# Expert tiles 36 to 38 of a mixture-of-experts layer put behind a test of the filled count

## The chip, the core and the metric

The kernel runs on one core of a Trainium2 chip, as one program. The metric is the device time of one execution in microseconds (us), lower is better. Times come from several executions of the same program; beside them one execution was recorded by the hardware profiler, and all views below are of that one.

The engines of a core run side by side and each works through its own queue of instructions: TensorE (PE; its loads of weights are shown as PEld), VectorE (DVE), ScalarE (ACT), GpSimd (POOL) and SyncE (SP). They wait for each other through semaphores. An engine's sequencer (shown with a q, POOLq) reads the queue and handles waits, register instructions and branches itself.

## What is computed

Input are 2048 tokens of 512 numbers, all in float32. Layer normalisation, a Mamba-2 block, a gated MLP, and then the part that matters here, a mixture of 8 experts of which each token uses two:

```python
x = x + _L0_attn_ref(_layernorm(x), ...)          # Mamba-2 and MLP
x = x + _L0_ffn_ref(_layernorm(x), Wr, Wg, Wu, Wd)

# _L0_ffn_ref, H = 512, I = 352, E = 8, K = 2
probs = softmax(x @ Wr)
topk_w, topk_idx = top_k(probs, K)
topk_w = topk_w / sum(topk_w)
g, u = x @ Wg[e], x @ Wu[e]
y[e] = (silu(g) * u) @ Wd[e]
out = sum over the token's two experts of weight * y[e]
```

The reference computes every expert for every token. The kernel computes a token's two experts alone.

## The kernel before

The work runs in blocks of tokens. The Mamba part (`mamba`, eight blocks of 256 tokens) and the MLP (`feed_forward`, four blocks of 512) are woven into each other; TensorE's order is the order of the program (`tc.manual_schedule` on PE, left by `in_order.close()` at line 1111). Each MLP block ends with `route`, which writes the normalised rows to memory (`xnd`, and `xnd1` for the first 1536 tokens), picks the two experts of each token and enters the tokens into a list for each expert.

**The tables.** An expert's list is cut into tiles of 128 tokens, and only as many tiles as it has are worked on. How many that is depends on the data, so the program lays out a fixed number, `NS`, and a table says which expert and which list a tile belongs to. The most that 4096 entries in eight lists can fill is `NS = (2 * T + NE * (P - 1)) // P` = 39 (line 38). `table` (line 924) is called twice:

- Table 1, for `NS1` = 10 tiles, after the first 1536 tokens. It counts full tiles only, so that these ten can be computed while the last MLP block still runs.
- Table 2, for the other `NS - NS1` = 29 tiles, after all tokens. Here an expert's tiles are its count over 128, rounded up, less those already used.

`upto_e` (line 939) is the running sum of tiles over the experts, so its last column is the number of tiles that the table fills. `exp_i` (lines 957 to 959) holds each tile's expert as an integer. A tile past the last list gets expert 7 and no tokens: its gather reads rows `T` to `T + 127`, which hold zeros, and its scatter adds zeros to the same spare rows of `out`. Such a tile takes the same instructions as a filled one.

**One expert tile** is these steps:

- `gather` (line 1012): POOL issues an indirect DMA that brings 128 rows into `xg`.
- `front` (1020): TensorE transposes them (`pt`, four matmuls, line 193) and ACT copies the result to `xgT` (line 195).
- `hidden` (1025): TensorE's sequencer reads the expert's number from `exp_i` (line 1027), and gate and up are computed from the weights in `ew` (line 1034). ACT takes the Silu (1038), DVE the product (1039).
- `turned` (1042): transposes of the product (`pht`), copied by DVE and ACT.
- `back` (1052): the down projection (`epd`, line 1055), scaled by the token's weight on DVE (`ey`, line 1060), and an indirect DMA from POOL that adds the rows to `out` (line 1061). Each such scatter waits for the one before to land.

`tiles` (line 1078) runs these for all tiles as a pipeline of two: while gate and up of tile s are computed, the product of tile s - 1 is transposed and projected down; gathers are issued two tiles ahead (`fetch`, line 1070). For the last tile the order changes so that the tile before is finished first (lines 1090 and 1095). `second` runs table 2 between the first tiles. Behind the last tile the program ends with a drain of each engine and two barriers of all engines, which the profile puts down to line 1174.

Of the kernel before, what the change touches and what calls it, by code (L numbers as in the profile page):

```python
# [9 lines left out]
I32 = mybir.dt.int32  # L10
# [5 lines left out]
P = 128  # L16
T = 2048
# [15 lines left out]
NE = 8  # L33
# [4 lines left out]
NS = (2 * T + NE * (P - 1)) // P  # L38

NS1 = 10  # L40
EW = NK * 2 * EI + len(ET) * D
EPS = 1e-5

# [6 lines left out]
def mamba_mlp_moe(ctx, tc, x, w_in, w_out, w_gu, w_down, par, wr, wg, wu, wd, out):  # L50
# [3 lines left out]
    nc = tc.nc  # L54

    def bc(ap, axis, n):
        ap = ap.unsqueeze(axis)
        shape = list(ap.shape)
        shape[axis] = n
        return ap.to_broadcast(shape)  # L60
# [9 lines left out]
    small_p = ctx.enter_context(tc.tile_pool(name="small_p", bufs=1, side="right"))  # L70
# [55 lines left out]
    upto = const.tile([P, NE, NE], F32, name="upto")  # L126
# [45 lines left out]
    def bank(kind, shape, name):  # L172
        pool, tag = use[kind]
        return pool.tile([P, *shape], F32, name=name, tag=tag)
# [138 lines left out]
    def finish(steps):  # L313
        while True:
            try:
                next(steps)
            except StopIteration as end:
                return end.value
# [226 lines left out]
    def mid(shape, name):  # L545
        return wk.tile([P, *shape], F32, name=name, tag="mid", bufs=3)
# [16 lines left out]
    def small(name, *shape):  # L563
        return small_p.tile([P, *shape], F32, name=name, tag=name)
# [340 lines left out]

    ew = pexp.tile([P, NE, EW], F32, name="ew")
    NG = NK * 2 * EI
# [16 lines left out]
    def table(n, name, used=None):  # L924


        pn = bank("tr", [NE], f"pn{name}")
        nc.tensor.matmul(pn, ones, before, start=True, stop=True)
        tiles, upto_e, gt, up8 = small("tiles", NE), small("upto_e", NE), small("gt", NE, NHI), small("up8", NE, NE)
        if used is None:  # L930
            nc.vector.tensor_tensor(gt, bc(pn, 2, NHI), bc(count_hi, 1, NE), ALU.is_ge)
            nc.vector.tensor_reduce(tiles, gt, AX.X, ALU.add)
            nc.vector.tensor_scalar_add(tiles, tiles, -1.0)
        else:
            nc.vector.tensor_tensor(gt, bc(pn, 2, NHI), bc(count_hi, 1, NE), ALU.is_gt)
            nc.vector.tensor_reduce(tiles, gt, AX.X, ALU.add)
            nc.vector.tensor_tensor(tiles, tiles, used, ALU.subtract)
        nc.vector.tensor_tensor(up8, upto, bc(tiles, 1, NE), ALU.mult)
        nc.vector.tensor_reduce(upto_e, up8, AX.X, ALU.add)


        step, goal = small("step", NE), small("goal", 1)
        nc.vector.tensor_scalar(step, tiles, -1.0, float(NHI), ALU.mult, ALU.add)
        nc.vector.tensor_scalar_add(goal, place[:, 0:1], -1.0)
        if used is not None:
            nc.vector.tensor_tensor(step, step, used, ALU.subtract)
            nc.vector.tensor_tensor(step[:, : NE - 1], step[:, : NE - 1], used[:, 1:], ALU.add)
            nc.vector.tensor_tensor(goal, goal, used[:, 0:1], ALU.subtract)
        past, exp_f, col = mid([n, NE], f"past{name}"), small("exp_f", n), small("col", n)
        nc.vector.tensor_tensor(past, bc(upto_e, 1, n), bc(count[:, :n], 2, NE), ALU.is_le)  # L950
        nc.vector.tensor_reduce(exp_f, past, AX.X, ALU.add)
        nc.vector.tensor_tensor(past, past, bc(step, 1, n), ALU.mult)
        nc.vector.tensor_reduce(col, past, AX.X, ALU.add)
        nc.vector.tensor_tensor(col, count[:, :n], col, ALU.add)
        sel = small("sel", n)
        nc.vector.tensor_scalar(sel, col, goal, None, ALU.is_equal)
        exp_i = small_p.tile([P, n], I32, name=f"exp_i{name}")
        nc.vector.tensor_scalar_min(exp_f, exp_f, NE - 1.0)
        nc.vector.tensor_copy(exp_i, exp_f)
        yield  # L960
        plt = bank("tr", [2, P], f"plt{name}")
        for a in range(2):
            nc.tensor.transpose(plt[:, a, :], lists[:, a, :], ident)
        lists_t = mid([2, P], f"lists_t{name}")
        nc.vector.tensor_copy(lists_t, plt)
        yield
        pi = bank("tr", [2, n], f"pi{name}")
        for a in range(2):
            nc.tensor.matmul(pi[:, a, :], lists_t[:, a, :], sel, start=True, stop=True)

        idx_f, tok_w = small("idx_f", n), small_p.tile([P, n], F32, name=f"tok_w{name}")
        idx = small_p.tile([P, n], I32, name=f"idx{name}")
        nc.vector.tensor_scalar(idx_f, pi[:, 0, :], 0.0, spare, ALU.is_equal, ALU.mult)
        nc.vector.scalar_tensor_tensor(idx_f, idx_f, -1.0, pi[:, 0, :], ALU.add, ALU.add)
        nc.vector.tensor_copy(idx, idx_f)
        nc.vector.tensor_copy(tok_w, pi[:, 1, :])
        done = None
        if used is None:

            done, start = small_p.tile([P, NE], F32, name=f"done{name}"), small("start", NE)  # L980
            nc.vector.tensor_tensor(start, upto_e, tiles, ALU.subtract)
            nc.vector.tensor_scalar_min(start, start, float(n))
            nc.vector.tensor_scalar_min(done, upto_e, float(n))
            nc.vector.tensor_tensor(done, done, start, ALU.subtract)
        return exp_i, tok_w, idx, done
# [4 lines left out]
    def routed(steps):  # L990

        nonlocal first
        yield from steps
        first = yield from table(NS1, "1")

# [12 lines left out]
    def of(s):  # L1008

        return (s, first, xnd1) if s < NS1 else (s - NS1, rest, xnd)  # L1010

    def gather(s):
        n, (_, _, idx, _), src = of(s)
        xg = row(f"xg{s}")
        nc.gpsimd.indirect_dma_start(  # L1015
            out=xg, out_offset=None, in_=src, in_offset=bass.IndirectOffsetOnAxis(ap=idx[:, n : n + 1], axis=0)
        )
        return xg

    def front(s, xg):  # L1020
        xT = wk.tile([P, NK, P], F32, name=f"xgT{s}", tag="a", bufs=4)
        transposed(xg, xT)
        return xT
# [18 lines left out]
    def turned(s, h):  # L1042

        pt = bank("tr", [len(ET), P], f"pht{s}")
        for m, (lo, n) in enumerate(ET):
            nc.tensor.transpose(pt[:n, m, :], h[:, lo : lo + n], ident)
        hT = wk.tile([P, len(ET), P], F32, name=f"ehT{s}", tag="a", bufs=4)
        nc.vector.tensor_copy(hT[:, 0:2, :], pt[:, 0:2, :])  # L1048
        nc.scalar.copy(hT[: EI - 2 * P, 2, :], pt[: EI - 2 * P, 2, :])
        return hT  # L1050

    def back(s, hT, w):
        pd = bank("d", [D], f"epd{s}")
        for m, (lo, n) in enumerate(ET):
            nc.tensor.matmul(  # L1055
                pd, hT[:n, m, :], w[:n, NG + m * D : NG + (m + 1) * D], start=(m == 0), stop=(m == len(ET) - 1)
            )
        y = wk.tile([P, D], F32, name=f"ey{s}", tag="row", bufs=5)
        n, (_, tok_w, idx, _), _ = of(s)
        nc.vector.tensor_scalar_mul(y, pd, tok_w[:, n : n + 1])  # L1060
        nc.gpsimd.indirect_dma_start(  # L1061
            out=out, out_offset=bass.IndirectOffsetOnAxis(ap=idx[:, n : n + 1], axis=0), in_=y, in_offset=None,
            compute_op=ALU.add,
        )

    AHEAD = 2
    rest = None
    got, xT = {}, {}

    def fetch(upto):  # L1070

        for s in range(min(upto + AHEAD, NS if rest else NS1)):
            if s not in got:
                got[s] = gather(s)
        if upto in got:
            xT[upto] = front(upto, got[upto])

    def tiles():


        fetch(0)
        yield
        last = None
        for s in range(NS):
            fetch(s + 1)
            steps = hidden(s, xT.pop(s))
            next(steps)
            if last:
                hT = turned(s - 1, last[0])
            if last and s == NS - 1:  # L1090
                back(s - 1, hT, last[1])
            now = finish(steps)
            yield
            if last:
                if s < NS - 1:
                    back(s - 1, hT, last[1])
                yield
            last = now
        back(NS - 1, turned(NS - 1, last[0]), last[1])

    def second():

        nonlocal rest
        yield from feed
        rest = yield from table(NS - NS1, "2", first[-1])

    work, steps = tiles(), second()
    next(feed)
    for _ in work:
        next(steps, None)  # L1110
    in_order.close()


# [64 lines left out]
```

## Time and profile before

| | us |
|---|---|
| median of 3 runs (lowest to highest) | 1582.76 (1581.46 to 1583.14) |
| the profiled execution | 1582.87 |
| its span, first to last instruction | 1580.9 |
| first read of an expert's number | 1239.5 |
| first gather, last gather issued | 1216.0, 1534.4 |
| last `ey` done | 1571.78 |

The difference of 2.0 us between the profiled execution and its span lies before the first and after the last instruction of the program. TensorE's granted clock over the whole span is 0.99 of full speed.

The costliest groups of the expert stage on the page (line, engine, operation, names and count; then busy us and mean ns of one; then the engine's idle time before them and what ended it):

```profile
L1034 PE MATMUL epg<-ew,xgT 128*128 x312 | 118.1, 460 | 0.4 <-issue 0.2
...
L1034 PE MATMUL epu<-ew,xgT 128*128 x312 | 117.8, 459 | 0.0
...
L1055 PE MATMUL epd<-ew,ehT 128*128 (+1 forms) x234 | 107.1, 593 | 1.0 <-DVE ehT L1048 1.0
...
L1015 POOL DMA_INDIRECT xg<-xnd,idx x39 | 38.9, 997 | 175.9 <-PE pt L193 173.8
...
L1061 POOL DMA_INDIRECT out<-ey,idx x39 | 61.9, 1588 | 66.8 <-DVE ey L1060 40.8
```

A float32 matmul is two passes in the records, so the four products over the 512 input columns are 8 records a tile for gate and 8 for up (312 = 39 x 8), and the three of the down projection 6 (234 = 39 x 6).

### The profile page before, as it was taken

How to read it: one execution, taken by the hardware profiler on the slowest of the kernel's cores; microseconds unless marked ns; L12 is line 12 of the kernel's file. 1: busy time of each engine (PE TensorE's matmuls, PEld its weight loads, DVE VectorE, ACT ScalarE, POOL GpSimd, SP SyncE). 2: the span in 40 equal slices, each digit the busy share in tenths (PEclk: the TensorE clock that was granted, in tenths of full speed). 3: DMA queues.
4: the chain of work that ended last, by engine and by line, in shares of the span. 5: the costliest groups of instructions: out<-in, count | busy, mean ns of one | idle time of the engine just before them, and what ended most of it. 6: DMA issues, size and time to landing. Idle time of an engine off the chain costs nothing. (4 is left out here: it accounts for less than half of the span.)

```text
span 1580.9 us, 19196 instructions
## 1 busy us (share of the span) xinstructions
PE 1537.3 (97%) x6303; PEld 1052.7 (67%) x6303; DVE 776.9 (49%) x2018; ACT 753.2 (48%) x1346; POOL 404.2 (26%) x510
## 2 busy tenths in 40 slices
PE   7899979999999999999999999999999999999997
PEld 6666666767666677767676777666777666555553
DVE  6776755754556464646555554434454352222221
ACT  3888796745663778457748543222211221111110
POOL 3442324333341212121212112011111123333331
PEclk8999989999999999999999999999999999999999
DMA  8443435544554553333344533238777233333332
GB/s 287 143 154 115 140 117 177 181 151 153 177 198 142 167 164 116 128 127 129 128 163 151 167 95 101 89 95 298 239 239 237 83 62 60 63 64 67 67 67 33
DMA packets 127456, 218.68 MB, mean 138 GB/s; under 512 B 11584, under 2 KB 71488, under 8 KB 127360
## 3 DMA queue, kind: packets, MB, share of 16 engines
q1 hardware_dynamic: 105088, 166.08, 33.1%
q0 software_dynamic: 8736, 20.45, 7.3%
q10 hardware_dynamic: 13536, 30.94, 5.1%
q8 instruction: 52, 0.85, 0.2%
q14 instruction: 44, 0.36, 0.1%
HBM read 176.01 MB, written 41.42 MB: 138 GB/s over the span
## 5 line engine op out<-in xcount | busy, mean ns | idle before, releaser
L685 PE MATMUL pd<-md,a 128*128 128x512 f32 x512 | 238.4, 592 | 0.0
L326 PE MATMUL pm<-hT,wi 128*128 128x256 f32 x768 | 188.9, 392 | 2.3 <-DMA wi<-in_w_in 2.3
L326 PEld LDWEIGHTS pm<-hT,wi 128*128 128x128 f32 x768 | 144.6, 195 | 27.9 <-issue 6.9
L686 DVE TENSOR_TENSOR r<-r,pd 128x512 f32<-128x512 f32 x128 | 87.6, 684 | 139.7 <-PE pd L685 139.0
L685 PEld LDWEIGHTS pd<-md,a 128*128 128x128 f32 x512 | 97.0, 190 | 74.1 <-issue 66.2
L347 DVE SCALAR_TENSOR_TENSOR ca<-pre,params,ca 128x256 f32<-128x256 f32 x288 | 135.0, 528 | 0.2
L701 PE MATMUL py<-h2T,ms 128*128 128x256 f32 x512 | 131.6, 379 | 1.6 <-POOL ms L527 0.8
L326 PE MATMUL pz<-hT,wi 128*128 128x256 f32 x512 | 118.9, 385 | 0.0
L1034 PE MATMUL epg<-ew,xgT 128*128 x312 | 118.1, 460 | 0.4 <-issue 0.2
L766 POOL TENSOR_TENSOR a<-a,up 128x256 f32<-128x256 f32 x64 | 47.3, 739 | 277.5 <-DVE up L760 240.4
L1034 PE MATMUL epu<-ew,xgT 128*128 x312 | 117.8, 459 | 0.0
L475 PE MATMUL po<-w_o,zs 128*128 128x512 f32 x256 | 112.8, 594 | 0.0
L406 ACT ACT_TABLE_LOAD x76 | 97.5, 1283 | 27.7 <-DVE ncum L274 19.2
L1055 PE MATMUL epd<-ew,ehT 128*128 (+1 forms) x234 | 107.1, 593 | 1.0 <-DVE ehT L1048 1.0
L701 PEld LDWEIGHTS py<-h2T,ms 128*128 128x128 f32 x512 | 95.6, 190 | 17.3 <-ACT up L740 1.6
L326 PEld LDWEIGHTS pz<-hT,wi 128*128 128x128 f32 x512 | 96.1, 193 | 15.6 <-issue 1.9
L406 ACT ACTIVATE cum<-cum,ncum 128x128 f32<-128x128 f32 x256 | 86.3, 393 | 7.9 <-POOL cum L300 4.3
L475 PEld LDWEIGHTS po<-w_o,zs 128*128 128x128 f32 x256 | 48.2, 190 | 57.0 <-issue 55.7
L1015 POOL DMA_INDIRECT xg<-xnd,idx x39 | 38.9, 997 | 175.9 <-PE pt L193 173.8
L1034 PEld LDWEIGHTS epu<-ew,xgT 128*128 128x128 f32 x312 | 59.3, 190 | 33.0
L1061 POOL DMA_INDIRECT out<-ey,idx x39 | 61.9, 1588 | 66.8 <-DVE ey L1060 40.8
L195 ACT COPY xgT<-pt 128x512 f32<-128x512 f32 x39 | 22.8, 587 | 117.7 <-PE pt L193 117.7
(248 smaller groups left out, 2567.7 us busy)
## 6 DMA issues: line engine op xcount, KB each, us to landing
wi<-in_w_in SPq DMA_DIRECT2D x80, 512.0 KB, 3.8
ms<-late SPq DMA_DIRECT2D x48, 512.0 KB, 3.6
mg<-early SPq DMA_DIRECT2D x48, 384.0 KB, 3.7
md<-in_w_down SPq DMA_DIRECT2D x64, 256.0 KB, 3.8
cum<-rowsd SPq DMA_DIRECT2D x32, 512.0 KB, 4.0
late<-ms ACTq DMA_DIRECT2D x16, 512.0 KB, 2.7
ec<-rowsd SPq DMA_DIRECT2D x60, 128.0 KB, 3.7
xnd<-xn ACTq DMA_DIRECT2D x28, 256.0 KB, 3.8
```

The lines of the kernel that those rows point to most:

```text
L326: nc.tensor.matmul(pm[:, m, :], w[:, k, m * P : (m + 1) * P], hT[:, k, :], start=(k == 0), stop=(k == NK - 1))
L347: nc.vector.scalar_tensor_tensor(ca, pre[:, m, k : k + TB], cw[:, k : k + 1], ca, ALU.mult, ALU.add)
L406: nc.scalar.activation(lt[:, half, i], lt[:, half, i], AF.Exp, bias=ncum[:, j, h : h + 1])
L475: nc.tensor.matmul(po, y[:, m, :], w_o[:, m, :], start=(m == 0), stop=(m == 7))
L685: nc.tensor.matmul(pd, a[:, j * P : (j + 1) * P], d, start=(m == 0), stop=(m == 1))
L686: nc.vector.tensor_tensor(rows[j], rows[j], pd, ALU.add)
L701: nc.tensor.matmul(ps, w[:, k], m[:, k], start=(first and k == 0), stop=(k == KH - 1), skip_group_check=True)
L766: nc.gpsimd.tensor_tensor(a[:, 1], a[:, 1], up, ALU.mult)
L1015: nc.gpsimd.indirect_dma_start(out=xg, out_offset=None, in_=src, in_offset=bass.IndirectOffsetOnAxis(ap=idx[:, n : n + 1], axis=0))
L1034: nc.tensor.matmul(ps, xT[:, k, :], w[:, lo : lo + EI], start=(k == 0), stop=(k == NK - 1))
L1055: nc.tensor.matmul(pd, hT[:n, m, :], w[:n, NG + m * D : NG + (m + 1) * D], start=(m == 0), stop=(m == len(ET) - 1))
L1061: nc.gpsimd.indirect_dma_start(out=out, out_offset=bass.IndirectOffsetOnAxis(ap=idx[:, n : n + 1], axis=0), in_=y, in_offset=None, compute ...
```

## The change

36 tiles stay as they were, in the same pipeline; `NSA` is their number. Table 2's `exp_i` gets one more column, into which the number of filled tiles of that table is copied (in table 1 as well, where nothing reads it). Behind the loop, every engine reads that number into a register and compares it with `NSA - NS1` = 26. If it is greater, tiles 36 to 38 are computed one after the other, each from its gather to its scatter; if not, all engines go past that block. The tables still lay out 39 tiles, so the lists of any input find their place.

```diff
+NSA = (2 * T + NE * (P // 2)) // P
...
-        exp_i = small_p.tile([P, n], I32, name=f"exp_i{name}")
+
+        exp_i = small_p.tile([P, n + 1], I32, name=f"exp_i{name}")
         nc.vector.tensor_scalar_min(exp_f, exp_f, NE - 1.0)
-        nc.vector.tensor_copy(exp_i, exp_f)
+        nc.vector.tensor_copy(exp_i[:, :n], exp_f)
+        nc.vector.tensor_copy(exp_i[:, n:], upto_e[:, NE - 1 :])
...
-        for s in range(min(upto + AHEAD, NS if rest else NS1)):
+        for s in range(min(upto + AHEAD, NSA if rest else NS1)):
...
-        for s in range(NS):
+        for s in range(NSA):
             fetch(s + 1)
...
-            if last and s == NS - 1:
+            if last and s == NSA - 1:
                 back(s - 1, hT, last[1])
...
-                if s < NS - 1:
+                if s < NSA - 1:
                     back(s - 1, hT, last[1])
                 yield
             last = now
-        back(NS - 1, turned(NS - 1, last[0]), last[1])
+        back(NSA - 1, turned(NSA - 1, last[0]), last[1])
...
     in_order.close()
+    filled = nc.values_load(rest[0][0:1, NS - NS1 :], min_val=0, max_val=NS)
+    with tc.If(filled > NSA - NS1):
+        for s in range(NSA, NS):
+            h, w = finish(hidden(s, front(s, gather(s))))
+            back(s, turned(s, h), w)
```

In the program built from it, TensorE, DVE, ACT and POOL each have the register read and a compare-and-branch behind their last instruction of tile 35, and SP behind its last load. Of the skipped block, TensorE has 99 instructions before its matmuls are split into passes, DVE 19, ACT 14, POOL 12, SP 1. Where the block is skipped, a short piece takes its place: on POOL three waits for earlier transfers and one instruction that raises the semaphores of the six skipped transfers, on the others one or two instructions that raise their own semaphores, so that the end finds the same counts on both ways. A branch to the closing drain and barriers follows.

## The prediction

> **What bounds the kernel now.** I read the page from the top: the shares of the engines, then the slices, to see which stage the change touches and what sets the pace there.
>
> ```profile
> PE 1537.3 (97%) x6303; PEld 1052.7 (67%) x6303; DVE 776.9 (49%) x2018; ACT 753.2 (48%) x1346; POOL 404.2 (26%) x510
> ...
> PE   7899979999999999999999999999999999999997
> ...
> PEclk8999989999999999999999999999999999999999
> ...
> q8 instruction: 52, 0.85, 0.2%
> q14 instruction: 44, 0.36, 0.1%
> ```
>
> TensorE is busy 97% of the span, at full clock in the last slices, and the only slack there is in the very last slice. The expert tiles fill the stretch from about 1239 us to the end, so the question is whether they go at TensorE's pace to the last one. The view of windows answers that (columns: stretch, its length, then busy time and count of PE, PEld, DVE, ACT, POOL, the clock, the DMA share and GB/s), and the timeline shows the period (start, length, what):
>
> ```profile
> 1347.69:1541.61 193.92, 193.92 (x697) 116.46 (x696) 40.72 (x72) 31.50 (x72) 61.90 (x48) 1.00 0.37 66
> ```
>
> ```profile
> 1315.37 0.60 PE L193 MATMUL pt<-ident,xg 128*128 128x128 f32 x4
> ...
> 1549.74 0.60 PE L193 MATMUL pt<-ident,xg 128*128 128x128 f32 x4
> ...
> 1571.03 0.75 DVE L1060 TENSOR_SCALAR ey<-epd,tok_w 128x512 f32<-128x512 f32 x1 [2.94 <-PE epd L1055]
> 1572.06 1.55 POOL L1061 DMA_INDIRECT out<-ey,idx  x1 [5.41 <-DVE ey L1060]
> ```
>
> In 193.92 us TensorE is busy for all 193.92: no other engine and no gather is waited for. The four transposes of a gathered tile come once a tile. Those at 1549.74 are of the last tile, number 38, since no gather follows; those at 1315.37 are 29 periods earlier. One tile takes (1549.74 - 1315.37) / 29 = **8.082 us**. The next two views are of what closes the program: all that bears the kernel's last line (engine, operation, shortest/median/longest ns, first and last start), and the chain that ended last.
>
> ```profile
> L1174 SPq EVENT_SEMAPHORE  x11: 17/28/38965, 1537.8 to 1580.8; - x11
> L1174 POOLq EVENT_SEMAPHORE  x4: 17/17/17, 1580.1 to 1580.8; - x4
> L1174 POOLq DRAIN  x3: 51/107/8227, 1571.8 to 1580.6; - x3
> ```
>
> ```profile
> 1565.10 1.55 DMA out<-ey,idx
> 1566.65 5.17 issue
> 1571.83 1.79 POOLq L1174
> ```
>
> The last scatter's descriptors are made by 1572.06 + 1.55 = 1573.61. POOL's drain stands behind it from 1571.83 for 8.23 us, to 1580.05; the first barrier event of POOL follows at 1580.1. So POOL's drain sets the end. Scatters of the last 40 us landed 4.7 us after their start, so this one is down at 1576.8, and the drain goes on 3.3 us past that. The other engines have long been done: the last `ey` is ready at 1571.78, 8.3 us before the barrier.
>
> **Is the condition true?** It is false if 36 tiles or fewer are filled. Routing the reference's own inputs by its own formula gives the experts 528, 490, 446, 505, 492, 582, 522 and 531 tokens. In tiles of 128, rounded up, that is 5+4+4+4+4+5+5+5 = 36. The first table takes 10 full ones (the first 1536 tokens fill 20 of them), so the second holds 26, and 26 > 26 is false. The nearest count to an edge is 505, seven under 512; rounding in the kernel would have to turn more than seven tokens of one expert. The block is skipped.
>
> **What goes.** Three tiles: in each 4 + 8 + 8 + 3 + 6 = 29 TensorE matmuls with their loads of weights, one gather, one scatter, the copies and the Silu. The loop keeps its form and its special case for the last tile moves with `NSA`, so the ramp-down is the same, three periods earlier: 3 x 8.082 = **24.25 us**, all on the engine that sets the pace. Beside other work, and worth nothing by themselves, are the DVE, ACT and DMA parts.
>
> **What comes, in the tables.** One DVE copy of one column in each table. The nearest row is the conversion `exp_i<-exp_f` at L959, 0.17 us. In table 2 it comes near 1301 us, where DVE sat idle 0.38 us before its next tile's copy, and its result is wanted much later: the first gather of the second list is issued at 1309.99, lands 3.4 us later by the median and is transposed at 1323.45. Table 1 is made during the last feed-forward block, with TensorE busy. Cost nothing, at most 0.2 us; without the cover 0.17 each.
>
> **What comes, at the end.** Each engine reads one register and takes a branch. On SP both stand behind its last load, after which it waits some 300 us for the end; on ACT and TensorE there is slack of some 9 us or more, on DVE 8.3. Only POOL's matter, since nothing but its drain is queued behind them, and the barrier waits for that drain. In order on POOL, behind the last scatter: the register read; a compare and branch over the 12 instructions of the skipped block; waits on six earlier scatters or gathers, all landed; one instruction that raises the skipped transfers' semaphores; a branch; the drain.
>
> ```profile
> L1027 PEldq TENSOR_LOAD <-exp_i x39: 297/682/1001, 1239.5 to 1553.8; - x39
> ```
>
> - The read: the nearest row is TensorE's own, 0.30 to 1.00 us, 0.68 in the middle.
> [...]
> - Raising the semaphores has one row, at the program's start, 0.03 us with nothing to raise. What it costs POOL with six to raise is not shown: between 0 and one scatter's descriptor time, 1.6 us.
>
> The sum is about 0.7 + 0.2 + 0.1 = 1.0 us of POOL's sequencer. The sequencer had reached the drain at 1571.83, while the scatter's descriptors ran to 1573.61; so the new work can lie beside them (cost 0), or wait for their end and push the drain back (cost 1.0, up to 1.0 + 0.2 + 1.6 = 2.8). Below nothing isn't possible, as the scatter and its landing stay. The drain ends after the landing, which nothing here moves, so I lean to the lower end and take **0.5 us**.
>
> [...]
>
> **The sum.** The profiled execution took 1582.87 us: its span of 1580.9 and 2.0 around it, which the change doesn't touch. 1582.87 - 24.25 + 0.5 = **1559.1 us**. The median of the three shown runs is 1582.76, 0.1 below, so the sum stands for a median too.
>
> **The rivals.**
> - *The end takes some of it back.* [...] For it: the drain's 6.4 us after the last descriptor is longer than the landing explains, so its rule is unknown. Against it: POOL's later two drains took 0.11 and 0.05 us, so a drain with nothing outstanding is short, and this one mainly waits for the transfer.
> - *The block is taken.* If one more tile is filled (37), all three are computed after the join, in one piece that cannot lie beside the others. POOL's branch comes about 1 us after its last scatter, at 1573.61 - 24.25 + 1.0 = 1550.4; the gather lands at 1553.8; the first tile costs 0.6 of transposes, 0.7 for the copy, 6.05 of gate and up, 0.68 waiting for Silu and product, 0.55, 0.52 and 2.85 of down, 11.95 in all, the two others about 10.7 each as their copies are hidden. TensorE ends at 1587.2, the tail of 9.9 us follows, and 2.0 around: about 1599 us, slower. It decides from one expert's list crossing one multiple of 128. For it: total 36 stands exactly on the edge. Against it: the counts above.
> - *The last tiles weren't worth a full period*, because some other engine paced them. The window above says no: full clock, no idle time up to the last.
>
> **How the numbers follow.** Skipped with a cost at the end of 0 to 2.8 us: 0.77. Skipped with more, up to 8: 0.17. Taken: 0.04. Something else: 0.02. The runs before lie within 1.7 us, so the range reaches from 1557.3 (no cost, a fast run) to 1564.0 (the first rival). What a measurement of this kernel can tell from no change is about 0.2%, 3.2 us: faster 0.94, same 0.02, slower 0.04.
>
> **What would show it.** Right: 36 gathers and 36 scatters; 6303 - 3 x 29 = 6216 matmuls; a period still of 8.08 us to the end; the last `ey` ready near 1571.78 - 24.25 = 1547.5; a register read, a branch and a drain on POOL, with the drain ending some 8.3 to 8.8 us after that `ey`. Wrong: 39 scatters, three of them after the branches; or more than 10 us between the last `ey` and the barrier; or a gap of TensorE near 1301 us.

## The result and the profile after

| | before | after |
|---|---|---|
| median, us (lowest to highest, 4 runs each) | 1582.11 (1581.02 to 1583.14) | 1558.39 (1557.46 to 1561.86) |
| profiled execution, us | 1582.87 | 1561.86 |
| its span, us | 1580.9 | 1560.2 |

The ratio of the medians is 0.9848, with a 95% interval of 0.9834 to 0.9863: 23.7 us less. The page of the changed kernel, the lines that answer to those shown of before:

```profile
PE 1514.4 (97%) x6216; PEld 1039.5 (67%) x6216; DVE 771.0 (49%) x2011; ACT 749.3 (48%) x1337; POOL 395.3 (25%) x504
...
PE   7899979999999999999999999999999999999996
...
PEclk8999989999999999999999999999999999999999
...
q8 instruction: 52, 0.85, 0.2%
q14 instruction: 46, 0.38, 0.1%
...
L1039 PE MATMUL epg<-ew,xgT 128*128 x288 | 109.1, 460 | 0.4 <-issue 0.4
...
L1020 POOL DMA_INDIRECT xg<-xnd,idx x36 | 35.8, 995 | 160.4 <-PE pt L196 158.4
```

The block was skipped: 36 gathers, and 6216 matmuls, which is 3 x 29 fewer. The matmul of gate and up still takes 460 ns, and the shares haven't moved. The queue q14, of the kind instruction, shows 46 packets in place of 44. Line numbers are those of the new file, three higher at the Mamba code and five at the tiles.

How long the stage of the expert tiles is can be read without what came before it: from its first gate matmul to its last `ey`. The timeline of before, and the one of after (start, length, engine, line, operation):

```profile
1243.16 0.86 PE L1034 MATMUL epg<-ew,xgT 128*128 x2 [0.24 <-issue]
```

```profile
1245.97 0.86 PE L1039 MATMUL epg<-ew,xgT 128*128 x2 [0.24 <-issue]
...
1549.63 0.75 DVE L1065 TENSOR_SCALAR ey<-epd,tok_w 128x512 f32<-128x512 f32 x1 [2.94 <-PE epd L1060]
1550.66 1.55 POOL L1066 DMA_INDIRECT out<-ey,idx  x1 [5.41 <-DVE ey L1065]
```

Before, the last `ey` started at 1571.03, so 327.87 us after the first gate matmul; after, 1549.63 - 1245.97 = 303.66. The stage is **24.21 us** shorter. The recorded run began it 2.81 us later than the one of before. All of that arose in the first 160 us, in code that the change doesn't touch; there, between 40 and 160 us, this run's granted clock was 0.96 against 0.99. The next recorded run of the same kernel began at 1244.11. So the late start is the run's own, and it makes up most of the 3.5 us by which the profiled execution lies above the median.

The end is where the change added work. Views of the changed kernel by line, 1117 (the register reads), 1118 (the branch and the piece for the skipped block) and 1184 (the close); columns as before, shortest/median/longest ns and first to last start:

```profile
L1117 POOLq TENSOR_LOAD <-exp_i x1: 504/504/504, 1550.4 to 1550.4; - x1
```

```profile
L1118 POOLq EVENT_SEMAPHORE  x3: 17/43/43, 1551.5 to 1551.6; - x3
...
L1118 POOLq COMPARE_BRANCH  x1: 53/53/53, 1551.0 to 1551.0; - x1
L1118 POOLq INC_SWDGE_SEM  x1: 1616/1616/1616, 1551.7 to 1551.7; - x1
```

```profile
L1184 POOLq EVENT_SEMAPHORE  x4: 17/17/17, 1559.4 to 1560.0; - x4
L1184 POOLq DRAIN  x3: 51/107/5946, 1553.4 to 1559.9; - x3
```

In POOL's order: the read at 1550.4, the branch at 1551.0 and the waits are all through by 1551.68, before the last scatter's descriptors are made (1550.66 to 1552.21). Only the instruction that raises the skipped transfers' semaphores sticks out. It is there from 1551.72 to 1553.34, 1.13 us past the descriptors, and the drain starts behind it at 1553.37. From the end of the last `ey` (1550.38) to POOL's first barrier event (1559.36) it takes 8.98 us, where before it was 1580.10 - 1571.78 = 8.32. So the stage gave 24.21 and the end took back 0.66. Outside the span there is a little more: the execution is longer than its span by 1.7 us in each of the nine runs of the changed kernel and by 1.8 to 2.1 in the runs of before. Why that is so is open.

### The profile page after: what moved, and what is told of

It is laid out like the page before. It is cut to its first block, busy times and chain, and to the rows that moved or that the text cites. A ratio compares the mean times of both kernels' runs of the same rounds, so it can differ in the third digit from the quotient of the medians.

```text
span 1560.2 us, 18963 instructions
## 1 busy us (share of the span) xinstructions
PE 1514.4 (97%) x6216; PEld 1039.5 (67%) x6216; DVE 771.0 (49%) x2011; ACT 749.3 (48%) x1337; POOL 395.3 (25%) x504
## 5 line engine op out<-in xcount | busy, mean ns | idle before, releaser
L1039 PE MATMUL epg<-ew,xgT 128*128 x288 | 109.1, 460 | 0.4 <-issue 0.4
L1039 PE MATMUL epu<-ew,xgT 128*128 x288 | 108.7, 459 | 0.0
L1060 PE MATMUL epd<-ew,ehT 128*128 (+1 forms) x216 | 98.9, 593 | 1.0 <-DVE ehT L1053 1.0
L411 DVE SCALAR_TENSOR_TENSOR cum<-cum,dt,psc 128x128 f32<-128x128 f32 x256 | 71.5, 340 | 9.7 <-PE psc L403 8.9
L749 ACT COPY a<-px 128x256 f32<-128x256 f32 x64 | 23.6, 369 | 109.5 <-PE px L704 90.9
L1039 PEld LDWEIGHTS epu<-ew,xgT 128*128 128x128 f32 x288 | 54.7, 190 | 30.5
```

Source lines behind the costliest of these rows:

```text
L411: nc.vector.scalar_tensor_tensor(lt[:, half, i], lt[:, half, i], dt[:, j, h : h + 1], psc[:, half, i], ALU.mult, ALU.mult)
L1039: nc.tensor.matmul(ps, xT[:, k, :], w[:, lo : lo + EI], start=(k == 0), stop=(k == NK - 1))
L1060: nc.tensor.matmul(pd, hT[:n, m, :], w[:n, NG + m * D : NG + (m + 1) * D], start=(m == 0), stop=(m == len(ET) - 1))
```

## The experiments

Each was compared with runs of the kernel before on the same chip. "End" is the time from the end of the last `ey` to POOL's first barrier event, "stage" that from the start of the first gate matmul to the end of the last `ey`; both are read from the timelines as above.

| kernel | median us (n) | ratio to before, 95% interval | stage us | end us |
|---|---|---|---|---|
| before (recorded run) | | | 328.62 | 8.32 |
| after (recorded run) | 1558.39 (4) | 0.9848 [0.9834, 0.9863] | 304.41 | 8.98 |
| the same again | 1558.62 (5) | 0.9843 [0.9830, 0.9857] | 304.38 | 8.99 |
| no branch | 1560.01 (5) | 0.9850 [0.9837, 0.9864] | 304.37 | 7.83 |
| block taken | 1599.21 (4) | 1.0098 [1.0077, 1.0119] | 344.74 | 8.33 |
| block without transfers | 1559.37 (5) | 0.9848 [0.9835, 0.9861] | 304.38 | 7.99 |
| 37 tiles | 1567.19 (4) | 0.9905 [0.9890, 0.9920] | 312.49 | 9.09 |
| column alone | 1582.50 (13) | 1.0002 [0.9994, 1.0011] | 328.62 | 8.31 |
| small test early | 1557.76 (5) | 0.9841 [0.9827, 0.9854] | 304.38 | 7.83 |
| whole block early | 1560.68 (4) | 0.9855 [0.9838, 0.9871] | 305.48 | 8.02 |
| 24 tiles (one run) | 1459.37 (1) | | 207.43 | 7.14 |

The runs without the branch and with it differ by less than their intervals, so differences of the order of 1 us are read from stage and end, which repeat to some 0.03 us between recorded runs of the same kernel.

**The changed kernel again.** No edit.

> The changed kernel once more, for a narrower interval and to see whether the profile's late start repeats. Three periods of TensorE less, 24.25 us, and some 0.7 us more at the end: 23.6 us below before, ratio 0.985. In the profile the last ey to POOL's first barrier event takes 9.0 us (8.3 before), the period is 8.08 us. If the 2.8 us by which the recorded run was late at its first expert tile belong to the change, they come again; if they are the run's own, they do not.

The end is 8.99 us and the stage 304.38 once more; the late start is not there (1244.11). The saving holds: 0.9843.

**No branch.** Against the changed kernel:

```diff
-        nc.vector.tensor_copy(exp_i[:, n:], upto_e[:, NE - 1 :])
...
-    filled = nc.values_load(rest[0][0:1, NS - NS1 :], min_val=0, max_val=NS)
-    with tc.If(filled > NSA - NS1):
-        for s in range(NSA, NS):
-            ...
```

> 36 tiles in the loop, no register read, no branch, no column for the count: tiles 36 to 38 are left out for any input that would fill them. If the test at the end costs what the profile suggests, the last ey to POOL's first barrier event is back at 8.3 us and the time is 24.25 us below before, 0.7 below the changed kernel. If the end's extra 0.7 us has another origin (the run, the moved tiles), it stays at 9.0 and the two kernels are equal.

The stage is the same, the end is shorter by 1.16 us, more than expected: it is below the 8.32 of before the change, not level with it. Its drain starts at the end of `ey` as before:

```profile
L1178 POOLq EVENT_SEMAPHORE  x4: 17/17/17, 1557.0 to 1558.0; - x4
L1178 POOLq DRAIN  x3: 51/107/7745, 1549.2 to 1557.5; - x3
```

7.75 us against 8.23 before the change, with the same scatter before it. So the test costs more at the end than the comparison with before shows, and the change has something beside it that gives 0.5 us back. The times of the two kernels (1560.01 and 1558.62) can't show this microsecond. Nor is all of it gained in the whole: from POOL's first barrier event to the last instruction it took 1.1 us here and 0.8 in the changed kernel, and outside the span 2.0 (median) against 1.7. With both, some 0.6 us of the 1.16 are left.

**The block taken.**

```diff
-    with tc.If(filled > NSA - NS1):
+    with tc.If(filled > NSA - NS1 - 1):
```

> The test compares with 25 in place of 26, so the block is taken. My sum for a block that is computed by itself: some 1599 us, 16 to 17 above before, with TensorE idle for about 4 us before the first of the three tiles and about 2 us in each. The rival, that a tile behind the branch costs what it costs in the pipeline: before plus the 0.7 us of the end, 1583.

1599.21 us, 15.5 above before: the branch is a matter of 41 us between its two ways, and it is decided by one tile. That rules out that a tile behind the branch costs what it costs in the loop. How the time comes together differs from my sum. TensorE's timeline:

```profile
1544.18 2.84 PE L1060 MATMUL epd<-ew,ehT 128*128 x6 [0.52 <-DVE ehT L1053]
1554.50 1.09 PE L196 MATMUL pt<-ident,xg 128*128 128x128 f32 x4 [7.47 <-DMA xg<-xnd,idx]
1556.32 1.54 PE L1039 MATMUL epg<-ew,xgT 128*128 x2 [0.73 <-ACT xgT L198]
...
1563.38 0.76 PE L1039 MATMUL epu<-ew,xgT 128*128 x2
...
1565.19 0.60 PE L196 MATMUL pt<-ident,xg 128*128 128x128 f32 x4
...
1568.56 0.76 PE L1039 MATMUL epg<-ew,xgT 128*128 x2
...
1572.70 0.76 PE L1039 MATMUL epu<-ew,xgT 128*128 x2
...
1574.52 0.60 PE L196 MATMUL pt<-ident,xg 128*128 128x128 f32 x4
```

and its stretches in the view of windows (the seventh figure after the length is the granted clock):

```profile
1554.50:1562.00 7.50, 6.77 (x14) 4.12 (x15) 0.00 (x0) 0.58 (x1) 0.94 (x1) 0.50 0.16 38
1562.00:1570.00 8.00, 7.25 (x25) 3.98 (x25) 1.70 (x3) 1.21 (x3) 0.21 (x1) 1.00 0.00 0
```

TensorE stands still for 7.47 us, not 4, until the first gather has landed. Then its granted clock is 0.50 for some 7.5 us: the four transposes take 1.09 us where they take 0.60 elsewhere, and gate and up take 7.82 (1556.32 to 1564.14) where they take 4.90 in the next tile (1568.56 to 1573.46). The two later tiles take 9.33 us each (1565.19 to 1574.52), less than my 10.7. Most of that lies in gate and up: my sum had 6.05 for them, which is eight times the 0.76 of one pair of matmuls, but the pairs overlap, and at full clock one starts every 0.59 us.

**A block without transfers.**

```diff
-        for s in range(NSA, NS):
-            h, w = finish(hidden(s, front(s, gather(s))))
-            back(s, turned(s, h), w)
+        nc.vector.memset(mid([EI], "never"), 0.0)
```

> The read and the branch stay on all engines, but the block behind the test holds one small DVE memset in place of tiles 36 to 38, which are left out for inputs that fill them. So no transfers' semaphores have to be raised when it is skipped. If raising them is what costs 0.7 us at the end, the last ey to the barrier takes 8.3 us as before the change; if the read and the branch cost it, 9.0 us.

```profile
L1182 POOLq EVENT_SEMAPHORE  x4: 17/17/17, 1555.1 to 1556.1; - x4
```

7.99 us: shorter than both expectations, 1.0 below the changed kernel, with the read and the branch still there on all engines. One reservation: with no transfers in the block, POOL's test came before its last scatter in the queue (the drain starts at 1547.2, as soon as the last `ey` is ready, with no read between), so this run alone does not show that read and branch are free behind the scatter. That is shown by the order on POOL in the changed kernel, where both end before the scatter's descriptors do (1551.04 against 1552.21).

**37 tiles.**

```diff
-NSA = (2 * T + NE * (P // 2)) // P
+NSA = (2 * T + NE * (P // 2)) // P + 1
```

> NSA is 37: one tile more in the loop, two behind the test. If a tile is worth one period of TensorE wherever the loop ends, this is 8.1 us above the changed kernel, 15.5 below before (two periods less, 0.7 more). If the three tiles at the end were worth less or more than the period, the step is another.

```profile
1241.92 0.56 PE L1039 MATMUL epg<-ew,xgT 128*128 x1 [0.24 <-ACT xgT L198]
...
1553.66 0.75 DVE L1065 TENSOR_SCALAR ey<-epd,tok_w 128x512 f32<-128x512 f32 x1 [2.94 <-PE epd L1060]
```

The stage is 8.11 us longer than that of the changed kernel, one period of 8.08. The time is 8.6 us higher, the ratio 0.9905. A tile was worth one period of TensorE at this step too.

With two tiles behind the test, four skipped transfers' semaphores have to be raised in place of six, and that took as long (1.67 us, from 1555.64, against 1.62): it was not a price for each transfer.

**The column alone.** The kernel before with the extra column of `exp_i` and its copy.

> The kernel before with the extra column of exp_i and its two copies, nothing else: 39 tiles, no test. Equal to before within 0.2 us, since DVE idles beside both copies. If they lie on the path of the tables, 0.1 to 0.4 us more, below what times can tell, but then TensorE's gap near the second table (0.46 us before) is longer.

Stage 328.62 and end 8.31, as before to the hundredth; ratio 1.0002. The copies cost nothing; in the run with the small test early, the next one, they took 0.15 us each.

**A small test early.**

```diff
     for _ in work:
         next(steps, None)
+        if rest and filled is None:
+            filled = nc.values_load(rest[0][0:1, NS - NS1 :], min_val=0, max_val=NS)
+            with tc.If(filled > NSA - NS1):
+                nc.vector.memset(small("goal", 1), 0.0)
     in_order.close()
```

> As the run with one DVE memset behind the test, but the test stands right behind table 2, in the middle of the tiles (tiles 36 to 38 are left out for inputs that fill them). If a skipped branch costs an engine only the 0.5 to 0.9 us of its sequencer, TensorE runs on from its queue or loses less than 1 us, and the end takes 8.3 us: 24 us below before. [...]

The stage is 304.38, the same as without any test. TensorE's stretch around the branch, at 1306.7 us:

```profile
1300.00:1320.00 20.00, 20.00 (x77) 12.54 (x78) 7.15 (x26) 3.11 (x7) 6.03 (x5) 1.00 0.33 65
```

It is busy for 20.00 of 20.00 us. The branch, 0.24 us of TensorE's sequencer while matmuls were queued, cost nothing here. The skipped block holds one DVE instruction, so TensorE has no semaphore to raise.

**The whole block early.** The same place, with tiles 36 to 38 behind the test, in buffers that are free by then:

```diff
-        xg = row(f"xg{s}")
+        xg = row(f"xg{s}") if s < NSA else wk.tile([P, D], F32, name=f"xg{s}", tag="row", bufs=5)
...
-        h = mid([EI], f"eh{s}")
+        h = mid([EI], f"eh{s}") if s < NSA else wk.tile([P, EI], F32, name=f"eh{s}", tag="h2T", bufs=1)
...
+            with tc.If(filled > NSA - NS1):
+                for s in range(NSA, NS):
+                    h, w = finish(hidden(s, front(s, gather(s))))
+                    back(s, turned(s, h), w)
```

> The changed kernel with the test and its block of tiles 36 to 38 right behind table 2, in the middle of the tiles, the block in buffers that are free by then. POOL raises the skipped transfers' semaphores there, not at the end, so the last ey to the barrier takes 7.8 us as without a branch, 1.15 less. But TensorE's own piece for the skipped block waits until all its earlier matmuls have ended before it raises its semaphore, so TensorE empties once: some 1 us idle near 1308 us. Sum: within 0.5 us of the changed kernel. [...]

The end is 8.02 us, 0.97 better, the stage 305.48, 1.10 worse: nothing is gained. The loss is where it was expected:

```profile
1308.56 0.53 PE L974 MATMUL pi<-sel,lists_t 128*128 128x29 f32 x4
1309.53 0.63 PE L196 MATMUL pt<-ident,xg 128*128 128x128 f32 x4 [0.45 <-PEq L1125]
1310.40 0.85 PE L1042 MATMUL epg<-ew,xgT 128*128 x2 [0.24 <-issue]
1311.09 0.76 PE L1042 MATMUL epu<-ew,xgT 128*128 x2
```

From the first of these matmuls to the first product of up it takes 2.53 us, and in the changed kernel, with no test there, 1.42 (1309.73 to 1311.15); that is the whole 1.10. TensorE waits 0.45 us for its own sequencer, which raises the first semaphore for the skipped block at 1309.13, when the last matmul before it has ended (1309.08), and another 0.24 before the next product; the rest, some 0.4 us, is that the matmuls on both sides of these waits no longer overlap. So the branch itself (0.37 us of the sequencer from 1307.3) was hidden in mid-stream, but making up the counts for the skipped block emptied TensorE once.

**24 tiles.** As without a branch, `NSA = 24`.

> As the run without a branch, but 24 tiles in the loop: tiles 24 to 38 are left out, so the tokens of the later experts miss their part. It is for the length of POOL's last drain. From the end of the last scatter's descriptors to the drain's end it was 6.44 us in the kernels with 39 gathers and 39 scatters and 5.96 us in the one with 36 of each, 0.08 us for each of the six. If the drain goes over all of POOL's indirect transfers of the program, 48 of them give 5.96 - 24 x 0.08 = 4.0 us. If it is a fixed time, or hangs on the last scatter's landing alone, it stays at 5.96 us.

```profile
L1178 POOLq DRAIN  x3: 51/107/7056, 1449.8 to 1457.4; - x3
```

Neither. (The stage is 15 periods shorter than that of before, 121.19 us or 8.08 for each.) From the end of the last scatter's descriptors the drain went on for 5.27 us; with 36 gathers and 36 scatters it was 5.96, with 39 of each 6.44. Fewer transfers, a shorter drain, but not by a fixed 0.08 us each: the 24 fewer give 0.69 us, where the last six gave 0.48.

## Why the prediction was right

- **The block is skipped.** Right, by the 36 gathers; and the run with the limit one lower shows that the count is exactly 26 in table 2, since there the block is computed.
- **24.25 us from three periods.** Measured 24.21 to 24.25 by the stage in five recorded runs with 36 tiles, and 8.11 for the step to 37. The last `ey` was ready at 1550.38 and not near 1547.5, by the late start of that run. The share of TensorE was the right reading: the other engines' work for these tiles, and the transfers, were worth nothing.
- **The copies cost nothing.** Right, 328.62 us of stage with and without them. TensorE has a gap near 1301 us, which was to be a sign of being wrong, but it has the same one before the change, where it waits for the tokens' lists: 0.46 us in both, up to 1300.93 and, before, up to 1298.12.
- **0.5 us at the end.** Measured 0.66, but two terms behind it were wrong, and that they nearly cancel is luck. Read, branch and waits, which I put at 0.9 us of sequencer, took 1.26, but were through before the scatter's descriptors and cost nothing. The 0.2 us in it for branches and waits was my estimate, and no run shows it: from the start of the branch to the end of the waits it took 0.69 (1550.99 to 1551.68), the branch itself 0.05. The raising of the semaphores, which I put at 0.1 us by a row where there was nothing to raise, ran until 1.13 us after the descriptors and pushed the drain back by that. Against it the drain became 0.46 us shorter (5.98 us from the end of POOL's last transfer instruction, 6.44 before), which I had excluded: "Below nothing isn't possible". And "the drain ends after the landing, which nothing here moves" doesn't hold, since the drain was pushed back while the landing wasn't (4.8 us after the issue by the median of the scatters, before and after). The drain's end came 8.94 us after the last `ey`, just outside the 8.3 to 8.8 that were to show the prediction right.
- **What stands behind the branches.** POOL's next instruction started 0.44 us after the end of its branch (1551.04 to 1551.48), DVE's 0.50 (1550.34 to 1550.84), and q14 had two packets more. In mid-stream TensorE was busy for 20.00 of 20.00 us around the branch of the small test. No run here skips more than three tiles.
- **The 2.0 us around the span.** Taken as untouched; they were 1.7 with the change, so some 0.3 us of the gain was not in the sum.
- **The rival of a taken block, 1599 us.** Measured 1599.21, but as a sum of misses that cancel. From its transposes to the end of its down projection the first tile took 14.2 us (1554.50 to 1568.72) and not 11.95, although the sum had set its gate and up too high: the halved clock added 3.4 us. The two others took 1.4 us less each. The first gather's landing was 0.6 us later than in the sum. TensorE's wait for it was no miss of the sum: the sum's own times (1553.8 for the landing, 1571.03 - 24.25 = 1546.8 for TensorE's end) make 7.0 us. The 4 us of the expectation didn't follow from them.
- **The rival of an end that takes some of it back.** The top of the range, 1564.0, lies 5.4 us above 1582.87 - 24.25. An end longer by that much was my estimate, and no run shows it: the end is 0.66 us longer.

What stays open is the rule of POOL's last drain. Counted from the end of POOL's last transfer instruction it takes 5.3 to 6.5 us here, less with fewer transfers before it (6.14 with 37 of each), but the number of transfers isn't all: the early-block run, with 36 of each, had 6.14 too and the one without transfers in the block 6.12, where the others with 36 had 5.96 to 5.98.

## What to carry to other kernels

When the pace of a stage is one engine's period (here TensorE's 8.08 us), padding costs whole periods, and a test that skips it is worth as many periods as it skips: put the price of the test against that, and look at which side of the edge the data lies. Price a test by what it leaves on the path: here the register read, the branch and the waits (1.26 us of POOL's sequencer) hid behind queued work, while making up the semaphores of the skipped block put about 1 us on the path, at the end on POOL (1.13) or in mid-stream on TensorE (1.10). A block behind a test is outside the pipeline, so if it can be taken on some inputs, work out that way too: here it was 41 us, 24 of them for three periods of TensorE, the rest idle time (7.47 us before the first tile), a clock of 0.50 (3.4 us) and tiles that no longer overlap (9.33 us each for 8.08).

## What was not expected of the hardware

- After 7.47 us without a matmul TensorE was granted 0.50 of its clock for some 7.5 us, and the transposes took 1.09 us for 0.60, the eight pairs of gate and up 7.82 for 4.90.
- Raising the semaphores of six skipped transfers took 1.62 us at the end, 1.13 of them past the last scatter's descriptors. In the early block it took 0.51 and was through at 1311.07, before the descriptors of the scatter ahead of it (1309.79 to 1311.36). The row at the program's start had shown 0.03. What makes it longer at the end is open.
- POOL's last drain was shorter in programs with fewer indirect transfers: from the last scatter's descriptors 6.44 us with 78 of them, 5.96 to 6.14 with 72, 5.27 with 48. Why is open.
